# First attention of a two-layer graph network with experts: a written instruction order from block 1 on, routing spread over more key steps, weight packing begun in block 0

## The chip, the cores and the metric

The kernel runs on one core of a Trainium2 chip. The metric is the device time of one execution in microseconds (us), lower is better. The engines are TensorE (PE, with its weight loads listed apart as PEld), VectorE (DVE), ScalarE (ACT), GpSimd (POOL) and SyncE (SP), which here only issues DMAs. One core does everything, so the time is set by the chain of work from engine to engine on this core.

## The reference

The network has 2708 nodes ("tokens") of 256 features, and two layers of graph attention followed by experts. Layer 0 is the one concerned.

```python
# graph attention of layer 0, added to x; its input is layernorm(x)
q, k, v = x @ Wq.T + bq, x @ Wk.T + bk, x @ Wv.T + bv
scores = q @ k.T / sqrt(256)
scores = where(adj > 0, scores, -9e15)          # adj: 2708 x 2708 int32
att = softmax(scores) @ v
x = x + elu(att)
# experts of layer 0, added to x; their input xt is layernorm(x)
probs = softmax(xt @ Wr + br)                   # 8 experts
top_p, top_idx = top_k(probs, 2)                # two per token
weights = top_p / sum(top_p)
xn = layernorm(xt)
y_e = gelu((xn * g_e + b_e) @ W1_e + b1_e) @ W2_e + b2_e      # hidden 1024
x = x + sum over the two chosen experts of weight * y_e
# layer 1: a second graph attention (additive scores) and 8 experts with hidden 512
```

All arithmetic is fp32, with the adjacency matrix kept as an fp8 mask inside the kernel.

## The kernel before

**Tiling.** The tokens are 22 tiles of 128 (`NT`; the last has 20 rows). First attention runs over query blocks `b`: five of 512 queries (four tiles each, `GROUP`), and a last one of 148 (`last`, b = 5). Each block runs over 22 key steps `k`. A key step does, in the order in which the code is written: `scores(b, k)`, that is two fp32 products into one of two PSUM buffers `s` (L568), the exponential on ScalarE (L580) and the product with the mask on VectorE (L583); then `attend` for the key step three earlier (`LAG` = 3), four products of 128x257 into four accumulators (L632); then a piece of the mask of the next block; then the line of routing steps.

**The mask of the next block.** `masks_of` loads five groups of the integer adjacency matrix per block on SP's queue (L414, 4 DMAs of 256 KB to a group; L418 and L422 with 8 smaller ones for the last block, whose unused columns are first set to zero, L410), compares them (L431, VectorE) and transposes the result (L437, VectorE). Group 0 and group 1 are asked for at k = 2 of the block before. The remaining 148 columns are loaded apart (`load_apart`, with the zeroing L449 for the last block). At a block's end the finished mask is stored to DRAM for layer 1 (`neighbours`, L741), which follows the last mask instruction L618.

**The line of routing steps.** When a block's accumulators are complete, `evict` copies them out (L657) and adds one generator per tile to `line`. `line.step()` is called once in each key step; it starts one waiting tile if `line.gap` steps have passed, and moves every running tile on by one `yield`. A tile's steps: divide by the softmax sum, form `neg` = min(raw, 0) (L644, VectorE) and its exponential (L645, ScalarE); the residual, the statistics of the norm and four gate dots (L261, VectorE); the normalised row (L281, VectorE, which waits for a GpSimd power L277), four more dots and the copy of the row for the second expert (L1218); the logits and the best two experts (L1238 to L1259); their exponential (L1261); two small products on TensorE that count tokens (L1264, L1265); the destinations and two indirect DMAs from GpSimd (L1282). Tiles from 16 on form their logits on TensorE instead of by dots.

**Other work placed in these key steps.** `gate_rows` (L251, L253) builds eight rows of the gate in block 0; `fold_gate` folds the second attention's gate in block 1, one `times_gate` at every fourth step: transposes (L294), a copy on ScalarE (L295), a product (L236), a copy on VectorE. `background` is a list of 50 DRAM-to-DRAM copies on SP's queue: 2 paddings, 32 pieces of layer 0's expert weights, 16 of layer 1's; after these, five loads of the stored masks for layer 1 (`mT`) are appended, which the first experts' stage issues in its odd slots. In the last block, `experts0.open` and `begin0` plan the first experts, in pieces (L1305 to L1394, small VectorE instructions), and fetch the first weights.

**Order.** SP's instructions run in written order in the whole kernel. TensorE, ScalarE and VectorE are ordered by the framework's scheduler in blocks 0 to 4, and by the code from the last block on:

```python
if b == last:
    line.gap = GROUP
    order0.enter_context(
        tc.manual_schedule(engines={PE, Activation, DVE}))     # names shortened
```

After first attention come the first experts (`experts0.run`), the second attention, the second experts and a final sum.

Of the kernel before, what the change touches and what calls it, by code (L numbers as in the profile page):

```python
# [22 lines left out]
D = 256  # L23
# [11 lines left out]
GROUP = 4  # L35
# [42 lines left out]
LAG = 3  # L78
# [26 lines left out]
def adj_ffn_kernel(ctx: ExitStack, tc: tile.TileContext, a: dict, out: bass.AP):  # L105
    nc = tc.nc
# [151 lines left out]
    def gate_dots(lg, x, r, experts, unused):  # L258

        for e in experts:  # L260
            nc.vector.scalar_tensor_tensor(  # L261
                unused, x, 1.0, wr_rows[:r, e],
                op0=ALU.mult, op1=ALU.mult, accum_out=lg[:r, e : e + 1],
            )

    def norm_stats(src, r):

        st = small.tile([P, 6], F32, name="ln_st")
        mv = small.tile([P, 2], F32, name="ln_mv")
        rs = small.tile([P, 2, 2], F32, name="ln_rs")  # L270
        nc.vector.bn_stats(st[:r], src)
        nc.vector.bn_aggr(mv[:r], st[:r])
        nc.vector.scalar_tensor_tensor(  # L273
            rs[:r, 0], once_twice[:r, 0], mv[:r, 1:2], once_twice[:r, 1],
            op0=ALU.mult, op1=ALU.add,
        )
        nc.gpsimd.tensor_tensor(rs[:r, 1], rs[:r, 0], minus_half[:r], ALU.pow)  # L277
        return mv[:r, 0:1], rs[:r, 1, 0:1], rs[:r, 1, 1:2], rs[:r, 0, 0:1]
# [35 lines left out]
    def over_sum(raw, r, n, total, alone):  # L314

        z = small.tile([P, 2], F32, name="z")
        nc.vector.tensor_scalar(alone, raw[:r, n : n + 1], 0.0, None, ALU.is_equal)
        nc.vector.scalar_tensor_tensor(
            z[:r, 0:1], alone, float(N), raw[:r, n : n + 1], op0=ALU.mult, op1=ALU.add
        )  # L320
        nc.vector.reciprocal(z[:r, 1:2], z[:r, 0:1])
        nc.vector.scalar_tensor_tensor(
            raw[:r, :n], total[:r], alone, raw[:r, :n], op0=ALU.mult, op1=ALU.add
        )
        return z[:r, 1:2]
# [47 lines left out]
    def layer0_attention(line):  # L373
        with ExitStack() as scope, ExitStack() as until_last:

            last = len(BLOCKS) - 1
# [12 lines left out]
            def of_block(b, name, shape, dtype, bufs=None):  # L389
                if b < last:  # L390
                    return wide.tile(shape, dtype, name=name, bufs=bufs)
                return pool.tile(shape, dtype, name=f"{name}_last", bufs=bufs)
# [6 lines left out]
            def masks_of(b, mT):  # L399

                b0, masks, last = b * BN, MASKS[b].words(mT), BLOCKS[b][1] < BN
                n = MASKS[b].padded // QUARTER

                def load(i):
                    adj = wide.tile([P, BN // QUARTER, P], I32, name="adj", bufs=3)
                    cols = a["adj"][:, i * BN : (i + 1) * BN].rearrange(
                        "r (g e) -> g r e", g=GROUP
                    )
                    if last:
                        nc.gpsimd.memset(adj[:, :n], 0)  # L410
                    for g in range(GROUP):
                        at = adj[g * QUARTER : (g + 1) * QUARTER]
                        if not last:
                            nc.sync.dma_start(  # L414
                                at, cols[g, b0 : b0 + BN].rearrange("(q n) e -> q n e", q=QUARTER)
                            )
                            continue
                        nc.sync.dma_start(  # L418
                            at[:, : n - 1],
                            cols[g, b0 : b0 + P].rearrange("(n q) e -> q n e", q=QUARTER),  # L420
                        )
                        nc.sync.dma_start(at[:TAIL, n - 1], cols[g, b0 + P : N])  # L422
                    return adj

                ahead = load(0)
                for i in range(WHOLE):
                    adj, ahead = ahead, load(i + 1) if i + 1 < WHOLE else None
                    size = n if last else GROUP
                    for h in range(0, n, size):
                        m = wide.tile([P, size, P], FP8, name="m_rows", bufs=2)  # L430
                        nc.vector.tensor_scalar(  # L431
                            m, adj[:, h : h + size], 0, None, ALU.is_gt, saturate=False
                        )
                        to = masks[:, i]
                        if not last:
                            to = to.rearrange("p (j q h) -> p h j q", j=GROUP, q=QUARTER)[:, h // size]
                        nc.vector.transpose(to, m.bitcast(I32))  # L437
                        yield

            def load_apart(b):  # L440

                n, rows_ = len(BLOCKS[b][2]), ROWS[BLOCKS[b][2][0]]
                adj = pool.tile([P, GROUP, REST], I32, name="adj_rest", bufs=1)
                apart = of_block(b, "apart", [P, n, REST], FP8)
                rest = a["adj"][b * BN : b * BN + BLOCKS[b][1], WHOLE * BN :]
                if b < WHOLE:
                    nc.sync.dma_start(adj, rest.rearrange("(p j) e -> p j e", j=GROUP))
                else:
                    nc.gpsimd.memset(adj, 0)  # L449
                    for j, t in enumerate(BLOCKS[b][2]):  # L450
                        nc.sync.dma_start(adj[: ROWS[t], j], rest[j * P : j * P + ROWS[t]])
                return apart, adj[:, :n]
# [184 lines left out]
            def finish(t, raw, total):  # L637
                r, xr = ROWS[t], xin.pop(t)
                rinv = over_sum(raw, r, D, total, alone[:r, t : t + 1])
                nc.vector.scalar_tensor_tensor(  # L640
                    raw[:r, :D], raw[:r, :D], rinv, bv_b[:r], op0=ALU.mult, op1=ALU.add
                )
                neg = rows0.tile([P, D], F32, name="neg", bufs=2)
                nc.vector.tensor_scalar(neg[:r], raw[:r, :D], 0.0, None, ALU.min)  # L644
                nc.scalar.activation(neg[:r], neg[:r], AF.Exp)  # L645
                yield
                nc.vector.scalar_tensor_tensor(
                    neg[:r], neg[:r], -1.0, raw[:r, :D], op0=ALU.add, op1=ALU.max
                )
                x1 = rows0.tile([P, D], F32, name="x1")  # L650
                nc.vector.tensor_add(x1[:r], neg[:r], xr[:r])
                yield from experts0.route(t, x1)
# [13 lines left out]
            folding = fold_gate(wide)  # L666
            for b, (b0, nb, ts_) in enumerate(BLOCKS):
                later_mask = iter(())
                if b == last:
                    line.gap = GROUP  # L670
                    order0.enter_context(
                        tc.manual_schedule(engines={
                            mybir.EngineType.PE,
                            mybir.EngineType.Activation,
                            mybir.EngineType.DVE,
                        })
                    )
# [3 lines left out]
                for k in range(NT):  # L681
# [38 lines left out]
                        g_next = queries(b + 1)  # L720
                    if k >= 2:
                        next(later_mask, None)
                    if background and k % 2 == 1 and b < last and (b > 1 or (b == 1 and k > 10)):
                        background.pop(0)()
                    if b > 0:
                        line.step()
# [2 lines left out]
                    if b == last and k == LAG + 2:  # L729
                        n = FULL_AFTER[experts0.early]  # L730
                        guess0 = experts0.open(
                            [i * (n // RING) * E // (n + GROUP) for i in range(AHEAD)] + [-1]
                        )
                        for _ in range(AHEAD):
                            next(guess0)
                        begin0 = experts0.begin()
                        for _ in range(6):
                            next(begin0)
                    if b == last and k in (LAG + 7, LAG + 11, LAG + 15):
                        next(begin0)  # L740
                nc.sync.dma_start(neighbours[b][:], mT)  # L741
                if b < last:
# [361 lines left out]
    class Experts:  # L1104
# [65 lines left out]
        def route(self, t, x, logits=None):  # L1170
# [4 lines left out]
            r = ROWS[t]  # L1175
            if own_norm:
                rows2 = routing.tile([P, 2, DROW], F32, name="row")
            else:
                rows2 = kept_pool.tile([P, 2, DROW], F32, name="row", bufs=6)
            mean, once, twice, _ = norm_stats(x[:r], r)  # L1180
# [34 lines left out]
            if own_norm:  # L1215
                if by_dots:
                    gate_dots(dots, x[:r], r, range(E // 2, E), rows2[:r, 1, :D])
                nc.vector.tensor_copy(rows2[:r, 1, :D], rows2[:r, 0, :D])  # L1218
            yield
            if not own_norm:  # L1220
                (nc.vector.tensor_copy if self.begun else nc.scalar.copy)(
# [24 lines left out]
            k = 2 if own_norm else E  # L1246
# [402 lines left out]
    background = []  # L1649
# [14 lines left out]
    line = Line(3)  # L1664
# [77 lines left out]
```

## Time and profile before

| | |
|---|---|
| time, median of 3 runs | 1215.17 us (1215.02 to 1219.6) |
| profiled execution, its own time | 1209.07 us |
| its span, first to last instruction | 1206.8 us |
| mean granted TensorE clock | 0.981 |
| TensorE busy | 1131.4 us, 94% of the span |
| weight loads busy | 914.3 us, 76% |
| VectorE busy | 621.0 us, 51% |
| ScalarE busy | 422.9 us, 35% |
| GpSimd busy | 419.9 us, 35% |
| first attention, blocks 1 to 5 | 122.4 to 497.15 us |
| first experts, second attention, second experts, sum | from about 497, 822, 997 and 1178 us |

Busy time of an engine is the union of its instructions' times; its difference to a window's length is idle time. A wait is the idle time of an engine ahead of an instruction, put down to the instruction elsewhere that released it: "PE s L568 <- ACT p L580" is TensorE waiting at line 568, which writes `s`, for ScalarE's line 580. Line numbers are those of the kernel before; in the changed one they are higher by one from L645 on.

### The profile page before, as it was taken

How to read it: one execution, taken by the hardware profiler on the slowest of the kernel's cores; microseconds unless marked ns; L12 is line 12 of the kernel's file. 1: busy time of each engine (PE TensorE's matmuls, PEld its weight loads, DVE VectorE, ACT ScalarE, POOL GpSimd, SP SyncE). 2: the span in 40 equal slices, each digit the busy share in tenths (PEclk: the TensorE clock that was granted, in tenths of full speed). 3: DMA queues.
4: the chain of work that ended last, by engine and by line, in shares of the span. 5: the costliest groups of instructions: out<-in, count | busy, mean ns of one | idle time of the engine just before them, and what ended most of it. 6: DMA issues, size and time to landing. Idle time of an engine off the chain costs nothing. (4 is left out here: it accounts for less than half of the span.)

```text
span 1206.8 us, 20877 instructions
## 1 busy us (share of the span) xinstructions
PE 1131.4 (94%) x6416; PEld 914.3 (76%) x6416; DVE 621.0 (51%) x2389; ACT 422.9 (35%) x1234; POOL 419.9 (35%) x524
## 2 busy tenths in 40 slices
PE   8989999999999998899999999998999998999990
PEld 5666666656666664699989989996999977899880
DVE  5465992865856747652222222224866777322214
ACT  3222221212122121443333323333776657544430
POOL 3011220120220303244333234433745557655540
PEclk9999999999999998999999999999999999999995
DMA  9293864976683389367868968634001527655557
GB/s 221 42 195 91 195 158 124 237 177 136 163 214 101 97 205 364 79 169 183 212 182 234 375 172 252 175 105 105 1 2 54 202 61 209 180 157 145 147 167 284
DMA packets 200717, 198.16 MB, mean 164 GB/s; under 512 B 92363, under 2 KB 183972, under 8 KB 194328
## 3 DMA queue, kind: packets, MB, share of 16 engines
q1 hardware_dynamic: 173530, 117.14, 39.6%
q0 software_dynamic: 26176, 76.85, 20.1%
q10 hardware_dynamic: 894, 2.77, 0.6%
q8 instruction: 53, 0.87, 0.3%
q14 instruction: 64, 0.52, 0.1%
HBM read 260.37 MB, written 66.15 MB: 271 GB/s over the span
## 5 line engine op out<-in xcount | busy, mean ns | idle before, releaser
L1533 PEld LDWEIGHTS mm<-xe,ring 128*128 128x128 f32 x2192 | 259.1, 193 | 25.4 <-DVE xe L1512 7.8
L1533 PE MATMUL mm<-xe,ring 128*128 128x128 f32 x2192 | 262.9, 277 | 16.3 <-DMA ring<-L_ffn_packed,weight_row 7.7
L1549 PE MATMUL acc<-ring,hT 128*128 128x256 f32 x1096 | 253.8, 382 | 0.7 <-ACT hT L1541 0.7
L1541 ACT ACTIVATE hT<-mm,ring 128x128 f32<-128x128 f32 x548 | 155.8, 369 | 273.2 <-PE mm L1533 139.4
L1549 PEld LDWEIGHTS acc<-ring,hT 128*128 128x128 f32 x1096 | 202.8, 192 | 25.0 <-ACT hT L1541 0.9
L632 PEld LDWEIGHTS acc<-v,p 128*128 128x128 f32 (+1 forms) x880 | 160.0, 190 | 63.4 <-issue 37.5
L568 PE MATMUL s<-g,xnT 128*128 128x512 f32 x420 | 202.3, 601 | 3.3 <-ACT p L580 3.3
L632 PE MATMUL acc<-v,p 128*128 128x257 f32 (+1 forms) x880 | 204.2, 384 | 0.6 <-DVE p L583 0.6
L1555 DVE SCALAR_TENSOR_TENSOR y<-acc,who,bias 128x256 f32<-128x256 f32 x92 | 44.4, 482 | 267.3 <-PE acc L1549 264.6
L277 POOL TENSOR_TENSOR ln_rs<-ln_rs,minus_half 128x2 f32<-128x2 f32 x88 | 66.1, 754 | 233.0 <-DVE ln_rs L273 210.0
L1282 POOL DMA_INDIRECT disp<-row,to x88 | 89.0, 1012 | 153.8 <-DVE to L1279 33.5
L1446 POOL DMA_INDIRECT ring<-L_ffn_packed,weight_row x92 | 97.5, 1059 | 107.7 <-PE acc L1549 68.5
L901 PE MATMUL acc<-parts,m 128*128 128x266 f32 x924 | 127.6, 296 | 0.0
L580 ACT ACTIVATE p<-s 128x512 f32<-128x512 f32 x105 | 62.0, 594 | 179.0 <-PE s L568 149.9
L901 PEld LDWEIGHTS acc<-parts,m 128*128 128x128 f32 x924 | 118.3, 187 | 4.4 <-ACT raw L928 0.9
L568 PEld LDWEIGHTS s<-g,xnT 128*128 128x128 f32 x420 | 77.3, 191 | 56.1 <-issue 48.2
L1568 POOL DMA_INDIRECT xd<-y,who x45 | 70.9, 1575 | 140.2 <-issue 71.3
L583 DVE SCALAR_TENSOR_TENSOR p<-p,mT 128x512 f32<-128x512 f32 x100 | 72.3, 725 | 58.3 <-ACT p L580 58.1
L868 ACT CAST m<-mT 128x512 fp32r<-128x512 fp8e4 (+4 forms) x168 | 72.2, 475 | 11.0 <-PE acc L901 7.6
L1512 DVE TENSOR_SCALAR xe<-xe_raw,ring 128x128 f32<-128x128 f32 x90 | 28.0, 360 | 65.7 <-DMA ring<-L_ffn_packed,weight_row 64.6
L1561 POOL DMA_INDIRECT xd<-y,who x47 | 46.9, 998 | 26.0 <-DVE y L1555 13.3
L261 DVE SCALAR_TENSOR_TENSOR row<-x,wr_rows 128x256 f32<-128x256 f32 x128 | 53.0, 416 | 0.3
(257 smaller groups left out, 1051.5 us busy)
## 6 DMA issues: line engine op xcount, KB each, us to landing
adj<-in_adj_dram SPq DMA_DIRECT2D x100, 256.0 KB
L_ffn_packed<-in_L_ffn_W_dram SPq DMA_DIRECT2D x32, 512.0 KB
xg<-disp SPq DMA_DIRECT2D x368, 32.0 KB
L_ffn_packed<-in_L_ffn_W_dram SPq DMA_DIRECT2D x32, 256.0 KB
neighbours<-mT SPq DMA_DIRECT2D x5, 1408.0 KB
mT<-neighbours SPq DMA_DIRECT2D x5, 1408.0 KB
ring<-L_ffn_packed SPq DMA_DIRECT2D x3, 2182.0 KB
xin<-in_x_dram SPq DMA_DIRECT2D x42, 128.0 KB
```

What stands on the lines that cost most here:

```text
L277: nc.gpsimd.tensor_tensor(rs[:r, 1], rs[:r, 0], minus_half[:r], ALU.pow)
L568: nc.tensor.matmul(ps[:kr, :nb], xnT[:, c, k0 : k0 + kr], g[:, c, :nb], start=(c == 0), stop=(c == DC - 1 and k < KEYS),)
L583: nc.vector.scalar_tensor_tensor(p, p, LARGEST, mask, op0=ALU.min, op1=ALU.mult)
L632: nc.tensor.matmul(accs[j][:r], p[keys, q0 : q0 + r], v[keys, k, :], start=(k == 0), stop=(k == NT - 1),)
L868: nc.scalar.copy(m[:, : q1 - q0], MASKS[b].of_key(mTs[b], k)[:, q0 - b * BN : q1 - b * BN],)
L901: nc.tensor.matmul(acc[:r], masks[t], parts[:, k, i], start=(k == 0 and i == 0), stop=False,)
L1282: nc.gpsimd.indirect_dma_start(disp[:], bass.IndirectOffsetOnAxis(ap=to[:r, j : j + 1], axis=0), rows2[:r, j], None,)
L1446: nc.gpsimd.indirect_dma_start(w, None, packed[:], bass.IndirectOffsetOnAxis(ap=self.weight_row[:, s : s + 1], axis=0), bounds_check=E * P ...
L1533: nc.tensor.matmul(ps[:, i, :], w[:, c * hidden + f * P : c * hidden + (f + 1) * P], xe[:, c, :], start=(c == 0), stop=(c == DC - 1),)
L1541: nc.scalar.activation(hT[:, f, :], ps[:, i, :], AF.Gelu, bias=w[:, b1 + f : b1 + f + 1])
L1549: nc.tensor.matmul(ps, hT[:, f, :], w[:, w2 + f * D : w2 + (f + 1) * D], start=(f == 0), stop=(f == hc - 1),)
L1568: start = nc.gpsimd.indirect_dma_start(xd[:], at, y, None, bounds_check=N - 1, oob_is_err=False, compute_op=ALU.add)
```

## The change

Eight edits, all but two of them in first attention:

1. TensorE, ScalarE and VectorE run in written order from block 1 on; before, from the last block on.
2. `line.gap` is five steps in blocks 0 to 3 and four from block 4 on; before, three, and four in the last block.
3. `background` copies are issued at odd key steps from k = 9 of block 0 on; before, from k = 11 of block 1 on. With 7 + 44 places up to the end of block 4, all 50 are issued there; before, 39 were, and 11 remained for the first experts' odd slots.
4. A `yield` stands between `neg` on VectorE and its exponential on ScalarE, so each tile takes one step more.
5. The copy of the row for the second expert (L1218) moves from VectorE to ScalarE.
6. Ahead of the last block's mask loads, VectorE sets one column of 128 (of five) to zero; before, GpSimd set all five.
7. The zeroing of `adj_rest` moves from GpSimd to VectorE.
8. In the last block, the six first pieces of `begin0` are issued one per key step from k = 5 to 10; before, all at k = 5. The three fetches of weights follow at k = 12, 16, 21; before, at 10, 14, 18.

```diff
@@ masks_of, load
                     if last:
-                        nc.gpsimd.memset(adj[:, :n], 0)
+                        nc.vector.memset(adj[:, n - 1], 0)
@@ load_apart
-                    nc.gpsimd.memset(adj, 0)
+                    nc.vector.memset(adj, 0)
@@ finish
                 nc.vector.tensor_scalar(neg[:r], raw[:r, :D], 0.0, None, ALU.min)
+                yield
                 nc.scalar.activation(neg[:r], neg[:r], AF.Exp)
                 yield
@@ layer0_attention, the loop over blocks
-                if b == last:
-                    line.gap = GROUP
+                line.gap = GROUP if b >= last - 1 else GROUP + 1
+                if b == 1:
                     order0.enter_context(
                         tc.manual_schedule(engines={
@@ the loop over key steps
-                    if background and k % 2 == 1 and b < last and (b > 1 or (b == 1 and k > 10)):
+                    if background and k % 2 == 1 and b < last and (b > 0 or k > 8):
                         background.pop(0)()
@@
                         begin0 = experts0.begin()
-                        for _ in range(6):
-                            next(begin0)
-                    if b == last and k in (LAG + 7, LAG + 11, LAG + 15):
+                    if b == last and LAG + 2 <= k < LAG + 8:
+                        next(begin0)
+                    if b == last and k in (LAG + 9, LAG + 13, LAG + 18):
                         next(begin0)
@@ Experts.route
-                nc.vector.tensor_copy(rows2[:r, 1, :D], rows2[:r, 0, :D])
+                nc.scalar.copy(rows2[:r, 1, :D], rows2[:r, 0, :D])
```

## The prediction

> **What bounds the kernel now.** I read the engine line of the page first: TensorE is busy for 1131.4 of 1206.8 us (94%), VectorE for 621.0 (51%). So the change can gain only what TensorE stands idle, or runs slowly after standing idle, in the stretch that it touches. The busy time by windows gives that stretch, first attention from block 1 (122.4 us) to the first expert product (497.15 us). The columns are start:end, length, busy us (instructions) of PE, weight load, DVE, ACT and POOL, TensorE clock, DMA share, GB/s.
> ```profile
> 119.00:203.00 84.00, 84.00 (x354) 55.34 (x354) 66.13 (x250) 18.41 (x42) 17.81 (x22) 1.00 0.59 140
> 203.00:286.00 83.00, 80.80 (x303) 51.33 (x303) 52.89 (x225) 16.99 (x38) 13.15 (x23) 0.98 0.79 188
> 286.00:365.50 79.50, 78.38 (x301) 50.33 (x301) 53.43 (x225) 17.10 (x38) 13.24 (x19) 1.00 0.79 190
> 365.50:443.00 77.50, 76.50 (x302) 49.98 (x301) 52.47 (x219) 16.97 (x38) 16.27 (x25) 1.00 0.53 126
> 443.00:497.00 54.00, 46.38 (x242) 27.71 (x240) 35.03 (x152) 10.90 (x42) 14.61 (x26) 0.94 0.78 273
> ```
> These are blocks 1 to 5. Blocks 1 to 4 have 0 + 2.2 + 1.1 + 1.0 us of idle TensorE in 324 us; the short last block has 7.6 in 54. The waits of TensorE say what these are, first for 119 to 443 us, then for 443 to 498 us (us in total, times, longest).
> ```profile
> PE s L568 <- ACT p L580: 3.3, 2, 2.2
> PE misc L1264 <- DVE sel L1259: 1.0, 3, 0.6
> ...
> PE s L568 <- ACT p_last L580: 5.1, 2, 4.7
> PE misc L294 <- DVE xn L281: 1.6, 2, 1.2
> PE mm L1533 <- ACT raw L657: 1.1, 1, 1.1
> ```
> The score product waits for ScalarE's exponential, which frees its PSUM buffer. Why was ScalarE late? Its own waits, 203 to 498 us:
> ```profile
> ACT neg L645 <- DVE neg L644: 43.2, 16, 7.4
> ACT p L1261 <- DVE p L1249: 29.1, 11, 7.5
> ```
> In both stalls ScalarE stood in its queue behind a routing exponential whose VectorE operand was late. In time order, TensorE at 251 to 257 us and 464 us, and ScalarE at 463.6 us:
> ```profile
> 251.00 1.96 PE L568 MATMUL s<-g,xnT 128*128 128x512 f32 x4
> 252.80 1.90 PE L632 MATMUL acc<-v,p 128*128 128x257 f32 x8
> 256.90 3.55 PE L568 MATMUL s<-g,xnT 128*128 128x512 f32 x4 [2.20 <-ACT p L580]
> ...
> 464.25 1.35 PE L568 MATMUL s<-g_last,xnT 128*128 128x148 f32 x4 [4.72 <-ACT p_last L580]
> ...
> 463.60 0.42 ACT L645 ACTIVATE neg<-neg 128x256 f32<-128x256 f32 x1 [7.26 <-DVE neg L644]
> ```
> After the idle 2.20 us the same four records took 3.55 instead of 1.96: the stall costs a second time, about 1.6 us. At 457.0 to 461.5 VectorE worked off 20 small instructions that plan the first experts (L1305 to L1394), issued together in one key step, and `neg` L644 came after them.
>
> **What the Trainium skill says.** "TensorE: Matmul & The Clock Gate", Part 1, has TensorE at half clock after an idle window of about 3.4 us, until a busy one. The trace agrees on half speed for one window, but shows it after 2.2 us of idle already; so I price an idle of 2 us or more at 1.7 us extra. "SBUF — State Buffer", Who interferes with whom: a VectorE instruction with two SBUF inputs blocks against a GpSimd one that reads SBUF. Here the mask product L583, 0.69 us as a rule, took 4.98 us while GpSimd built `wr_rows` (L253, from 124.7 us, 4.72 us):
> ```profile
> 124.98 4.98 DVE L583 SCALAR_TENSOR_TENSOR p<-p,mT 128x512 f32<-128x512 f32 x1 [0.37 <-ACT p L580]
> ```
> "DMA: Bandwidth & Descriptors", Latency and other measured facts, puts a DMA's fixed cost at about 2 us. The last-block mask load agrees roughly: the last of its 8 issues at 414.7, the compare at 417.2, after a mask product that had kept VectorE until then.
>
> **The change part by part**, against the profiled execution (1209.07 us, of which 2.3 lie around the span). A key step costs TensorE 3.45 us (scores 1.72, values 1.73).
>
> *Stalls of blocks 1 to 4 that go.* With five steps between tiles (four in block 4) and one more between `neg` and its exponential, VectorE is no longer asked for two tiles' heavy steps at once: 128 gate dots of 0.42 us and all else stay, spread evenly. ScalarE's operand is then a step old. Gone: 3.3 + 1.0 + 1.7 = **-6.0 us** (-6 to -3; the sel waits could stay).
>
> *Gate fold in block 1.* In written order, three times a transpose, ScalarE's copy and the product with G follow each other on TensorE with nothing between; the scheduler had put a score product there. The nearest row is the transposes in block 0 that wait for ScalarE, 0.73 us: 3 x 0.73 = **+2.2** (1 to 4).
>
> *Start of block 1.* `gate_mean` (3.84 us on VectorE at 120.4) and the 4.98 us above now stand ahead of later VectorE work in order: sum 8.8 us, against three steps of slack, 10.4 us, less what the evictions and exponentials take. **+2** (0 to 5).
>
> *Block 2:* **+0.4** (0 to 2), the sel wait of a tile. *Block 3.* The first mask group is compared at k=2 in written order, 6.9 us into the block; the scheduler had put it off to 224.8 us in block 2. It lands some 11.6 us after the last mask instruction of the block before (201.85 to 213.5), because the neighbours' store and packing copies lie ahead on SP's queue. Of the copies one more per block is ahead now. I take 2.2 us idle and half of a clock dip: **+3** (0 to 6).
>
> *Block 4.* Here the mask groups of the last block need a cleared column before their DMAs. GpSimd did that, early:
> ```profile
> SPq L741 <- DVE mT L618: 67.0, 4, 21.9
> SPq L418 <- POOL adj L410: 18.0, 1, 18.0
> ```
> Now VectorE clears (128 of 640 columns; 0.15 to 0.4 us each, by its small rows, GpSimd's took 0.64) and so the clear, 8 issues of 0.37 us (3.0) and 2 us of landing stand between two VectorE instructions of the same order. Walked through from the block's start: mask product 2 ends at 9.9; clears; issues of group 0 to 13.2, of group 1 to 16.1; compare 0 at 15.2, transposed 16.0; the tile's first step (1.8) to 17.8; product 3, clear 2 at 18.7, issued by 21.7; compare 2 at 23.7 to 24.5; third tile step (3.6) to 28.1; product 5, compare 3, then the normalised row at 30.2. That is what ScalarE's new copy L1218 (0.29 us on VectorE, some 0.4 on ScalarE) waits for, with exponential 6 behind it, and score product 8 behind that. It is due at 8 x 3.45 = 27.6 and comes at 31.2: 3.6 idle. SP's other entries at these steps (packing, x loads, the separate mask) add an estimated 1.3. The sel of this tile is then 1.4 late for L1264, and a clock dip follows, 1.7: **+8** (2 to 13). In blocks 1 to 3 the copy costs nothing, as long as VectorE is within a step of TensorE.
>
> *Last block.* The planning pieces, one per key step, no longer precede `neg` together: 5.1 us of stall and about 2.6 of slow clock go. But 35 us of VectorE work remain in some 46 us, and each key step is short, so about 3.2 us of that returns as waits for VectorE: **-4.5** (-9 to +1). With the pieces, the three weight fetches move 2, 2 and 3 key steps later, with their POOL issues; before, the first expert product waited 1.1 us for an eviction and for no weights, so I price them at 0, and at up to 3 us if a fetch becomes the last to land (in the next item's range). A tile's two POOL scatters move with its steps, a step later and up to a block's end; the last tile of a block then ends in the next one, at no cost while POOL is busy for 16 of 78 us.
>
> *Packing begun in block 0:* seven copies beside loads that feed block 0, where the DMA share is 0.64: **+0.5** (0 to 3). *First experts:* 11 leftover copies are gone from their first slots, activation-table loads are a few more: **-0.5** (-3 to +2). *The separate mask's clear* belongs to block 4's walk.
>
> Sum: -6.0 + 2.2 + 2 + 0.4 + 3 + 8 - 4.5 + 0.5 - 0.5 = **+5.1 us**, 1214.2 on the profiled execution's own time. That one is 6.1 us under the median of the runs (1215.17; 1215.02 to 1219.6), so against the median: 1220.3.
>
> **The rivals.**
> *Order holds (faster).* VectorE's lag stays inside the three-step slack, block 4's loads land before their compares (score product 8 not late, which needs the normalised row before 27.6 us), and the last block keeps its 7.7. For it: VectorE has 52 of 80 us of work in these blocks. Against: written order makes it wait for DMAs that the scheduler went around. -6 + 2.2 + 1 - 7.7 and nothing else: -10.5, 1204.7.
> *A wash (same).* Block 4's stall is half as large or the last block gains all: within 3 us of 1215.
> *Every block pays (slower than forecast).* Late first groups and the neighbours' order stall blocks 2, 3 and 4 alike, 6 us each with their dips, and the last block gains nothing: -6 + 4.2 + 18 = +16, 1231. It decides once the lag of VectorE at a block's end is above one step.
> That the change doesn't do what it says is no rival: the written order fixes the moves.
>
> **Chances.** 0.5% (6.1 us) is about what a measurement of this kernel can tell from no change: 1209.1 to 1221.3. Forecast 0.40, which splits 0.19 within and 0.21 above, since 1220.3 lies near the upper bound; order holds 0.27; wash 0.07; every block pays 0.26. From these: faster 0.27, within 0.26, slower 0.47. The forecast's own range is 1214 to 1228. The range 1204 to 1236 reaches to the value of the faster rival and past that of the last one by its unknown start of block 1 (+5); half of the faster rival and the far tail of the last are left out.
>
> **What would show it.** Right: no idle at 254, 323 and 459 us; in block 4 `s L568 <- ACT p L580` near step 8 and VectorE's `m_rows L431` waiting for the adj DMA; three waits of the gate fold's products for `gT L295` in block 1; a last block under 52 us instead of 54. Wrong: block 4 still 77 us long, or a block 1 or 2 longer by over 5 us, or the first experts starting late by waits on DMA.

## The result and the profile after

The changed kernel takes 1227.46 us (median of 9 runs, 1222.59 to 1232.41), the kernel before 1217.33 (9 runs, 1212.69 to 1222.05). The ratio is 1.009, with an interval of 1.0063 to 1.0117: slower by about 11 us. The forecast was slower by 5 us, with 0.47 for slower; the time lies in the stated range.

The engine line of the page after. TensorE's work is the same 6416 matmuls; VectorE's busy time rose by 26 us although 16 instructions left it.
```profile
PE 1135.5 (93%) x6416; PEld 914.3 (75%) x6416; DVE 647.0 (53%) x2373; ACT 432.9 (35%) x1260; POOL 425.6 (35%) x518
```
The busy time by windows of the changed kernel, cut at the last score product of each block (columns as in the prediction):
```profile
119.90:209.90 90.00, 84.26 (x336) 54.25 (x324) 67.94 (x218) 18.89 (x42) 16.44 (x17) 0.98 0.65 161
209.90:290.80 80.90, 78.63 (x311) 50.22 (x300) 62.41 (x231) 17.72 (x42) 15.46 (x22) 1.00 0.77 188
290.80:373.70 82.90, 78.93 (x312) 50.21 (x300) 62.40 (x231) 17.74 (x42) 15.27 (x21) 1.00 0.78 186
373.70:462.60 88.90, 79.36 (x314) 51.56 (x302) 58.78 (x229) 18.03 (x45) 16.29 (x24) 0.94 0.52 137
462.60:513.00 50.40, 46.73 (x260) 28.11 (x248) 34.91 (x157) 12.53 (x47) 16.15 (x26) 1.00 0.63 226
```
The same cuts in the kernel before give 81.7, 82.5, 79.7, 77.4 and 56.2 us, up to the first expert product. So block 1 lost 8.3 us, block 3 3.2, block 4 11.5; block 2 gained 1.6 and the last stretch 5.8. The first expert product comes at 513.0 instead of 497.1, 15.8 us later. The first experts then win 3.8 back (318.4 to 314.6 us). The two profiles differ by 18.4 us in all, 8.3 more than the medians do: the profiled execution of before was 8.3 us under its median. Of the 18.4 us, 7.6 lie in the second experts, whose code is untouched: they took 176.7 us there and 184.3 here, and spread from 176.2 to 184.4 in the kernels of this study.

What TensorE waits for in the changed kernel, 119 to 443 us:
```profile
PE s L568 <- ACT p L580: 15.8, 4, 9.5
PE misc L236 <- ACT gT L295: 3.5, 3, 2.5
PE acc L632 <- DVE raw L658: 2.2, 1, 2.2
```
The old waits (254, 323, 459 us, and the sel waits) are gone. New ones begin at 134 us (2.2), 187 (2.5), 238 (2.3), 312 (1.7), 321 (2.3) and 402 us (9.5). ScalarE's own waits, 203 to 513 us, name what kept the exponentials:
```profile
ACT p L580 <- PE s L568: 56.4, 28, 3.5
ACT row L1219 <- DVE row L261: 54.1, 10, 6.5
ACT row L1219 <- issue: 40.8, 6, 15.5
```
The moved copy is now the first reason why ScalarE stands still. Where the profile names what released it, that is L261, a gate dot, in all but one of the cases, and not the normalised row L281. The dots write their unused products into `rows2[:r, 1]`, the row that the copy fills; so the copy must come after the dots of its own key step. Block 4 in time order, first ScalarE, then VectorE (without three of the four dots), then TensorE:
```profile
411.25 0.41 ACT L1219 COPY row<-row 128x256 f32<-128x256 f32 x1 [15.54 <-issue]
411.57 1.08 ACT L580 ACTIVATE p<-s 128x512 f32<-128x512 f32 x2
```
```profile
404.22 0.17 DVE L410 MEMSET adj<- 128x128 int32 x1
408.27 0.49 DVE L431 TENSOR_SCALAR m_rows<-adj 128x640 fp8e4<-128x640 int32 x1 [3.88 <-DMA adj<-in_adj_dram]
408.80 0.34 DVE L437 STREAM_TRANSPOSE mT_last<-m_rows 128x160 int32<-128x160 int32 x1
409.07 0.37 DVE L281 TENSOR_SCALAR row<-x,ln_mv,ln_rs 128x256 f32<-128x256 f32 x1
...
410.75 0.42 DVE L261 SCALAR_TENSOR_TENSOR row<-x,wr_rows 128x256 f32<-128x256 f32 x1
```
```profile
412.21 3.78 PE L568 MATMUL s<-g,xnT 128*128 128x512 f32 x4 [9.54 <-ACT p L580]
```
The chain begins on VectorE: wait for a mask group, compare, transpose, normalise, four dots; then ScalarE's copy, its exponential, and TensorE after 9.54 us, at half clock (3.78 us for four records). VectorE waited three times in this block for such a load, 10.5 us in all.

### The profile page after: what moved, and what is told of

It reads as the page before. It is cut to its first block, busy times and chain, and to the rows that moved or that the text cites. A ratio compares the mean times of both kernels' runs of the same rounds, so it can differ in the third digit from the quotient of the medians.

```text
span 1225.3 us, 20889 instructions
## 1 busy us (share of the span) xinstructions
PE 1135.5 (93%) x6416; PEld 914.3 (75%) x6416; DVE 647.0 (53%) x2373; ACT 432.9 (35%) x1260; POOL 425.6 (35%) x518
## 5 line engine op out<-in xcount | busy, mean ns | idle before, releaser
L568 PE MATMUL s<-g,xnT 128*128 128x512 f32 x420 | 202.1, 602 | 15.8 <-ACT p L580 15.8
L583 DVE SCALAR_TENSOR_TENSOR p<-p,mT 128x512 f32<-128x512 f32 x100 | 68.2, 684 | 53.5 <-ACT p L580 53.5
L261 DVE SCALAR_TENSOR_TENSOR row<-x,wr_rows 128x256 f32<-128x256 f32 x128 | 54.9, 429 | 3.3
L431 DVE TENSOR_SCALAR m_rows<-adj 128x512 fp8e4<-128x512 int32 (+1 forms) x105 | 43.0, 421 | 22.3 <-DMA adj<-in_adj_dram 21.2
```

The source lines that it names most:

```text
L568: nc.tensor.matmul(ps[:kr, :nb], xnT[:, c, k0 : k0 + kr], g[:, c, :nb], start=(c == 0), stop=(c == DC - 1 and k < KEYS),)
L583: nc.vector.scalar_tensor_tensor(p, p, LARGEST, mask, op0=ALU.min, op1=ALU.mult)
```

## The experiments

The theories: **A**, the copy on ScalarE turns VectorE's lag into idle TensorE. **B**, the loads of the last block's mask, cleared, loaded and compared within a step or two in written order, make block 4 long. **Rivals:** written order costs by itself; the spread line or the packing costs. Ratios are to the kernel before, with 95% intervals; the changed kernel's is 1.009. The median of before itself lay at 1217.1, 1211.4 and 1210.8 us in the three sets, so ratios are compared.

**Copy back on VectorE.**
```diff
-                nc.scalar.copy(rows2[:r, 1, :D], rows2[:r, 0, :D])
+                nc.vector.tensor_copy(rows2[:r, 1, :D], rows2[:r, 0, :D])
```


> The changed kernel, with the copy of the row for the second expert back on VectorE. Theory A (the copy on ScalarE is what turns VectorE's lag into idle TensorE, since it also waits for the gate dots that write into the same row ahead of it): the idle 2.3 us of TensorE in blocks 2 and 3 (238 and 321 us) and 2.5 us at 187 us go, the 9.5 us in block 4 falls to 4 or less; 12 us less than the changed kernel, about 1215. Theory B (the round trip of clear, load and compare on VectorE in written order is the cause, whoever stands behind it): block 4 stays over 86 us long, and only 5 to 7 us go, about 1221.

Measured: 1219.99 us, 1.0018 (1.0002 to 1.0035), 0.7% less than the change. The idle at 238 us is gone, and those at 187 and 321 us fall to 0.5, as A says. But block 4 is still 86.1 us, and what TensorE waits for there is another instruction:
```profile
PE misc L1265 <- DVE sel L1260: 7.8, 1, 7.8
```
Without the copy, VectorE's lag in block 4 reaches TensorE by the counting products of the routing. So A holds for blocks 1 to 3, B for block 4.

**Clears back on GpSimd.**
```diff
-                        nc.vector.memset(adj[:, n - 1], 0)
+                        nc.gpsimd.memset(adj[:, :n], 0)
@@ load_apart
-                    nc.vector.memset(adj, 0)
+                    nc.gpsimd.memset(adj, 0)
```


> The changed kernel, with the two clears ahead of the last block's mask loads back on GpSimd. Theory B: block 4 falls from 88.9 to 78 or 79 us, blocks 1 to 3 stay; 10 us less, about 1217. Theory A: the copy still waits for the dots of its own step, so 2.3 us of idle stays in block 4 as in blocks 2 and 3; 7 to 8 us less with the clock dip, about 1220.

Measured: 1224.41 us, 1.0076 (1.0045 to 1.0106), which doesn't stand clear of the change. Block 4 falls from 88.9 to 83.6 us only, with one wait of 5.3 us left. Both theories had asked for more: who clears is less than half of the block's loss. Most of this gain doesn't reach the end of first attention in this profile, because blocks 2 and 3 take 1.6 and 1.9 us more than in the changed kernel's, though no edit touches them: in each of them TensorE ran at half clock for 3.4 us after an idle that passed without it there (see "Half clock" below).

**Both taken back.** The two diffs above together.

> The changed kernel with both taken back, the copy on VectorE and the clears on GpSimd. If A and B are two causes that add only where they meet (block 4), this is 16 us less than the changed kernel, about 1211, and about 6 under the kernel before, because the last block's 6 us are kept. A rival (written order costs by itself, in the gate fold and the late first mask groups): blocks 1 and 3 keep 5 and 3 us more than before, about 1217.

Measured: 1213.65 us, 0.9973 (0.9957 to 0.9988). Blocks 1 to 4 take 87.3, 79.6, 81.9 and 81.6 us. The time lies between the two expectations, and just under the kernel before. Blocks 1 and 3 keep 5.6 and 2.2 us above before, as the rival says. In block 4 VectorE still waits for three mask loads, 7.3 us in all, with the clears on GpSimd, and TensorE waits for what VectorE does after the last of them:
```profile
PE misc L1265 <- DVE sel L1260: 3.9, 1, 3.9
```

**Written order from the last block only.**
```diff
-                if b == 1:
+                if b == last:
                     order0.enter_context(
```


> The changed kernel with the written order from the last block on, as before; all other edits stay. If written order is needed for each of the losses: blocks 1 to 4 take 82, 82, 80 and 77 us as before and the last block 44, about 1211. If the spread line, the packing in block 0 or the copy on ScalarE cost by themselves: over 1217.

Measured: 1223.84 us, 1.0057 (1.003 to 1.0083). Blocks 2 to 4 are short (78.4, 79.6, 79.9), block 1 takes 84.4, but the last block takes 66.7 us, at a mean clock of 0.80. Its TensorE waits:
```profile
PE misc L294 <- DVE xn L281: 6.2, 2, 4.6
PE acc L632 <- DVE p_last L583: 4.7, 1, 4.7
PE misc L1265 <- DVE sel L1260: 4.3, 3, 3.5
```
The first expectation missed. The time is that of the second one, but blocks 1 to 4 together take 1 us more than in the kernel before: the loss isn't there. The scheduler put VectorE's last clear of a mask group at 435.7 us and the last compare at 450.3, into the last block: work of block 4 had been handed on. With the scheduler in these blocks the other edits together are slower than the kernel before; this run doesn't say which of them moved the clears so late.

**Mask groups of the last block at every third step.**
```diff
-                    if k >= 2:
+                    if k >= 2 and (b + 1 != last or k % 3 == 2):
                         next(later_mask, None)
```


> The changed kernel with one edit: in block 4 the five mask groups of the last block are compared at every third key step (2, 5, 8, 11, 14) and no longer at five steps in a row; clears stay on VectorE, the copy on ScalarE. Theory A and B together (block 4 is long because VectorE waits in order for a load that was asked for only a step before): block 4 falls from 88.9 to 80 or 81 us, with 2.3 us of idle left that the copy causes, as in block 3; about 8 us less than the changed kernel. Rival (the clears' engine or the ScalarE copy alone decide): block 4 stays over 85 us.

Measured: 1212.25 us, 0.9998 (0.998 to 1.0016), 0.9% less than the change by one line. Block 4 takes 78.0 us; what is left of its waits:
```profile
PE s L568 <- ACT p L580: 1.4, 1, 1.4
```
The clears are still on VectorE and the copy is still on ScalarE. VectorE's waits for mask loads in block 4 fall from three (10.5 us) to one, that of group 0, whose load and compare still stand in one key step:
```profile
DVE m_rows L431 <- DMA adj<-in_adj_dram: 3.9, 1, 3.9
```
So the cause in block 4 is the distance in key steps from the load to its compare. With three steps between them and the clears on VectorE, none of the four other loads is waited for; with one step, moving the clears to GpSimd was worth 5.3 us.

**The dots' products into a dead tile.**
```diff
-                yield from experts0.route(t, x1)
+                yield from experts0.route(t, x1, dump=neg)
@@ Experts.route, and the same for the second four dots
-                gate_dots(dots, x[:r], r, range(E // 2), rows2[:r, 1, :D])
+                gate_dots(dots, x[:r], r, range(E // 2), dump[:r])
```


> The changed kernel with one edit: the gate dots leave their unused products in the dead tile neg and not in the second expert's row, so that the copy on ScalarE waits for the normalised row alone and not for the four dots after it (1.85 us). Theory A: the idle 2.3 us in blocks 2 and 3 fall under 0.6 us each, and that at 187 us to 0.7; block 4's 9.5 falls by 2; 6 to 8 us less than the changed kernel, as with the copy on VectorE. Rival (the copy costs because ScalarE's queue waits for VectorE at all): nearly no change, over 1225.

Measured: 1211.72 us, 0.9998 (0.9982 to 1.0013). Blocks 1 to 4 fall by 2.0, 2.5, 2.5 and 2.5 us against the change, 9.5 together, with the copy where the change had put it. ScalarE now waits for the row itself. TensorE's wait at 238 us is gone, and those at 187 and 321 us shrink to 0.5 each. The third wait in the second line below, of 0.9 us, is the one that was 1.7 at 312 us, behind the exponential of `neg`:
```profile
ACT row L1219 <- DVE row L281: 66.4, 14, 14.2
```
```profile
PE s L568 <- ACT p L580: 9.8, 3, 8.3
```
The 8.3 us in block 4 stay, since they are B's. This settles A: not the copy on ScalarE costs, but its wait for four dots of the same step.

**Only the planning pieces spread.**
```diff
                         begin0 = experts0.begin()
-                        for _ in range(6):
-                            next(begin0)
-                    if b == last and k in (LAG + 7, LAG + 11, LAG + 15):
+                    if b == last and LAG + 2 <= k < LAG + 8:
+                        next(begin0)
+                    if b == last and k in (LAG + 9, LAG + 13, LAG + 18):
                         next(begin0)
```


> The kernel before with one edit: the planning pieces of the first experts one per key step. If the spread alone gave the last block's gain, the last block falls from 50.2 to 45 us (end of block 4 to the last score product), and the kernel is 6 us faster than before, 1211. If the block gains because written order hands it over without a backlog on VectorE, as the run with the late order suggests, it gains under 2 us.

Measured: 1214.49 us, 1.0028 (1.0008 to 1.0048). The last block falls by 3.0 us (50.2 to 47.2), half of the change's 6, so neither expectation holds whole. The first experts wait longer at their start, so that nothing is gained:
```profile
PE mm L1533 <- DVE xe L1512: 6.6, 1, 6.6
```

**Only the written order, in the kernel before.**
```diff
                 if b == last:
                     line.gap = GROUP
+                if b == 1:
                     order0.enter_context(
```


> The kernel before with one edit: written order on TensorE, ScalarE and VectorE from block 1 on, nothing else (line gap 3, copy on VectorE, clears on GpSimd, planning pieces together). If written order alone carries the loss of blocks 1 and 3 (gate fold, late first groups) and closer routing adds VectorE lag: blocks 1 to 4 take 88, 82, 83 and 84 us, the last block 50; about 15 us more than before. If it is harmless without the copy and the clears: within 5 us of before.

Measured: 1248.4 us, 1.0305 (1.0255 to 1.0355). Blocks 1 to 4 take 98.1, 87.7, 90.7 and 84.4 us. The longest waits of ScalarE and of TensorE:
```profile
ACT neg L645 <- DVE neg L644: 143.3, 20, 10.8
```
```profile
PE s L568 <- ACT p L580: 19.8, 12, 2.4
```
Without the extra `yield`, ScalarE waits for VectorE's `neg` of the same key step in every one of the 20 tiles, with the next score exponential behind it. It did so 20 times in the kernel before too, but for 53.3 us in all; in written order it is 143.3. Written order alone is thus more than twice as dear as expected, about 37 us; the seven other edits bring back about 26 of them. The wider gap is measured below, in another kernel; what the extra step brings by itself was not measured.

**All found waits mended.** Copy on VectorE; block 4's groups at every third step; group 0 of every block loaded at k = 2 and compared from k = 5 on; the gate fold split over two steps and begun at k = 6; the two query products one step apart. The diff shows the main lines; `apart` is true for every block.
```diff
@@ masks_of
                 ahead = load(0)
+                if apart:
+                    yield
@@ times_gate, called with yield from
             to_columns(turned, src, P)
+            yield
@@ the loop over key steps
-                    if b == 1 and k % GROUP == 0:
+                    if b == 1 and k >= 6 and k % 2 == 0:
-                        g_next = queries(b + 1)
-                    if k >= 2:
+                        g_next = queries(b + 1, None, [0])
+                    if k == NT - 5 and b + 1 < len(BLOCKS):
+                        queries(b + 1, g_next, [1])
+                    if k == 2 or (k >= 5 and (b + 1 != last or k % 3 == 2)):
                         next(later_mask, None)
```


> The changed kernel with five mends: copy on VectorE; masks of block 4 at every third step; in every block the first mask group loaded at k=2 and compared from k=5 on; the gate fold's product two key steps after its transposes, and the fold begun at k=6, clear of GpSimd's wr_rows; the two query products one key step apart. If these waits are what written order costs, blocks 1 to 4 take 81, 78.5, 79 and 77.5 us, the last 44, and first attention ends about 16 us before the changed kernel's 513 less a little: 491. Time about 1206, 11 under before. If written order costs by itself (VectorE's instructions overlap less), it stays near 1213, as the run with copy and clears taken back.

Measured: 1194.65 us against 1211.4, 0.9851 (0.9828 to 0.9873). The windows of blocks 2 to 4 have no idle TensorE left:
```profile
203.10:281.40 78.30, 78.30 (x306) 50.36 (x300) 63.27 (x233) 17.25 (x38) 14.61 (x21) 1.00 0.75 193
281.40:359.80 78.40, 78.40 (x309) 50.40 (x304) 63.59 (x234) 17.24 (x38) 14.76 (x21) 1.00 0.81 197
359.80:435.80 76.00, 76.00 (x313) 50.13 (x303) 61.39 (x240) 17.05 (x40) 16.68 (x24) 1.00 0.62 160
```
VectorE is as busy here as in the changed kernel (63 us of 78), and it no longer matters: it waits for no mask load in first attention (five times and 21.2 us in the changed kernel), and TensorE's waits there are 5.2 us in all (25.1). The rival, that written order costs by VectorE's smaller overlap, falls. First attention ends at 485.8, 27 us before the changed kernel's and 11 before the old one's. The five mends were not measured one by one in this kernel, and whether the scheduler's order would gain as much with the same mends was not run.

**Mended, with the copy on ScalarE and the dots into `neg`.** The copy as in the change, and the diff of the dead tile.

> The mended kernel with the copy on ScalarE as in the change, and the dots' unused products in neg. If the copy was harmful only by its wait for the dots, this is as fast as the mended kernel or up to 2 us faster, since VectorE has 20 copies of 0.29 us less. If any wait of ScalarE for VectorE in the same key step costs: 3 us or more slower.

Measured: 1191.05 us, 0.9824 (0.9789 to 0.9858): the fastest by its median, not separable from the mended one. The second expectation, 3 us or more slower, is out. Moving the copy costs nothing, once its hidden wait is gone.

**Mended, with a tile started every third step.**
```diff
-                line.gap = GROUP if b >= last - 1 else GROUP + 1
+                line.gap = GROUP if b == last else GROUP - 1
```


> The mended kernel with a tile started every third key step in blocks 1 to 4 as before, and not every fifth or fourth. If the wider spacing is needed, steps of two tiles meet on VectorE again: some 5 to 10 us of TensorE idle at the block starts. If written order with the extra step is enough, the same time as mended.

Measured: 1211.81 us, 0.9994 (0.9969 to 1.0019); blocks 1 and 2 take 93.1 and 83.0 us instead of 83.1 and 78.4. The spacing is worth about 1.4%, more than expected. TensorE's longest waits, 119 to 502 us:
```profile
PE misc L1271 <- DVE sel L1266: 10.9, 5, 3.2
```

**Mended, with the packing begun in block 1.**
```diff
-                    if background and k % 2 == 1 and b < last and (b > 0 or k > 8):
+                    if background and k % 2 == 1 and b < last and (b > 1 or (b == 1 and k > 10)):
```


> The mended kernel with packing begun in block 1 as before (11 pieces left to the first experts). If the packing in block 0 is neutral, as priced: the same within 3 us. If the leftover pieces disturb the first experts, these take 3 to 4 us longer than mended's 314.4.

Measured: 1199.85 us, 0.9897 (0.9852 to 0.9943), with an interval that overlaps that of mended. Its first experts take 321.1 us against 314.4: longer, as the second expectation says, and by more than its 3 to 4 us. TensorE's longest wait in the first experts, of this kernel and then of the mended one:
```profile
PE mm L1540 <- DVE xe L1519: 6.4, 5, 1.6
```
```profile
PE mm L1540 <- DVE xe L1519: 2.8, 2, 1.7
```
Half of the 6.7 us is in this wait; the rest isn't named by a line. The other kernels agree: in the four that leave 11 pieces the first experts take 318 to 322 us, in the ten that leave none 312 to 318. In blocks 0 and 1 the early packing costs 1.4 us together here (the end of block 1 comes at 203.0 against 201.7).

## Why the prediction was right, and where it was wrong

- **Sign and cause.** Slower, by waits of written order, block 4 first: right. The old stalls are gone as priced (-6.0). The total, +5.1, was under half of the measured one, about +11. The block figures below are net of the old stalls (3.9 us in block 2, 1.1 in block 3, 1.0 in block 4).
- **"In blocks 1 to 3 the copy costs nothing, as long as VectorE is within a step of TensorE."** This is the step that failed. The copy was taken to wait for the normalised row. It waits for the dots after it too, as they share its target; with the dots elsewhere, blocks 1 to 4 are 9.5 us shorter. Predicted and measured for blocks 1 to 4: +9.6 and +21.4. The copy's 9.5 are most of the gap.
- **Block 4, +8:** measured +11.5. The wait stands at score product 8, behind the copy, as walked. The idle was 9.5 us and not 3.6 + 1.3: the normalised row came 33.4 us into the block (409.07, from 375.65) instead of 30.2, because VectorE waited 10.5 us for three loads, and the dots stood behind it. The clear was only a part of the cause: on GpSimd it gives 5.3 us back, and with the clears on VectorE and three steps' distance the block takes 78.0.
- **Gate fold, +2.2:** 3.5 us idle; 1.5 with the copy back, so a turn cost 0.5 and not 0.73, and the copy added the rest. After the longest of these idles, 2.5 us, TensorE ran at half clock from 189.6 to 193.0 us.
- **Start of block 1, +2:** 2.2 us idle, so the size is right, but by luck: another instruction than the one named caused it. Not L583 but the gate fold's L213 met GpSimd's `wr_rows`, and the evictions behind it came late. The Trainium skill, "SBUF — State Buffer", Who interferes with whom, says that a VectorE instruction with two SBUF inputs contends with a GpSimd one that reads SBUF. L213 has two, and took 4.81 us where the same instruction just before it took 0.42; it ended 0.3 us after GpSimd's (130.05 to 134.87):
```profile
130.34 4.81 DVE L213 SCALAR_TENSOR_TENSOR junk<-wfc,wdst_b 128x256 f32<-128x256 f32 x1
```
- **Block 3, +3:** net +3.2, in part by luck. 1.7 us idle stand behind a first mask group for which VectorE waited 6.3 us, as said; the other 2.3 us are the copy's, which had no price there, and no half clock followed.
- **Last block, -4.5:** -6.0, of which spreading the planning pieces brings 3.0 by itself. **Packing in block 0, +0.5:** +0.3. **First experts, -0.5:** -3.8, mis-sized: copies left to their slots cost more than was priced.
- **Half clock.** A price of 1.7 us for every idle of 2 us was too simple. After 9.5 us idle, the 3.4 us from 412.0 ran at 0.50 and the next 3.4 at 0.57. After the idles of 2.3 us at 238 and 321 the blocks' clocks show none (1.00). But in the run with mask groups at every third step, which changes nothing in blocks 2 and 3, slow stretches follow the same two idles, and the blocks take 82.5 and 85.3 us instead of 80.9 and 82.9 (0.7 of it is a longer idle in block 3):
```profile
241.40:244.80 3.40, 3.16 (x4) 1.51 (x5) 3.04 (x12) 0.97 (x4) 0.00 (x0) 0.50 1.25 215
```
The slow stretches of a trace begin on a grid of 3.41 us that lies elsewhere in each execution. Counted over blocks 1 to 4 of all fourteen traces, a full-speed grid step in which TensorE was idle for more than 2.0 us was followed by a slow one in 22 of 22 cases, from 1.9 to 2.0 us in 3 of 5, and under that in none. So an idle of 2.3 us costs a slow step or not by where it falls on the grid.

## What to carry to other kernels

In an order written out by hand, an engine's queue is only as early as its latest operand: put at least one step between two engines' halves of a piece of work, and several between a load and its use, before taking the scheduler away. Look for tiles that are only dumps: a second writer of a dump makes a wait that no data asks for. And where a change of several edits comes out slower, find its waits and mend them before dropping it; here a kernel in the same order, with five mends, became 1.5% faster than the kernel before.

## What was not expected of the hardware

VectorE's busy time rose by 26 us in written order, though its instructions did not get longer. From block 1 to the first expert product their durations add up to 331.6 us before and 332.5 us after, but the union of their times is 259.5 and 286.4 us; with only the order changed, the figures are 335.5 and 290.3. (L583's mean falls from 725 to 684 ns because the one instance of 4.98 us, which met GpSimd, is gone.) In the kernel before, the next instruction of an independent chain often starts before the one ahead has ended: L640 starts 0.34 us after the dot at 244.15, which takes 0.42. In written order a tile's chain stands together, dot after dot, and the dot after the one at 238.27 starts 0.46 us later. The mended kernel keeps this (a union of 291.0 us) and is the faster one, so here it cost nothing.
